# Values of two masked head groups in one 256-wide product, a new order of the filling work, and single weight buffers

## The chip, the cores and the metric

The kernel runs on one core of one Trainium2 chip. The metric is the device time of one execution in microseconds (us). Before the change it is 3708.43 us, the median of 3 runs (3707.75 to 3712.06). TensorE, VectorE, ScalarE and GpSimd are called PE, DVE, ACT and POOL, as in the profile; SP is the engine whose queue issues most loads.

## What is computed

Four attention layers act one after the other on `x` [4 batches, 512 queries, 256 channels]; each attends to the same context [4, 1024 keys, 512]. All of it is float32. Layers 0, 2 and 3 are "masked" layers of 16 heads of 64 channels:

```python
q, k, v = x @ Wq, ctx @ Wk, ctx @ Wv              # 1024 wide each, split into 16 heads of 64
logits = q . k * 64 ** -0.5 + col_bias            # the bias is nonzero at four token columns
x = softmax(logits) @ v (heads joined) @ Wo + bo + x
```

Layer 1 is "grouped": an RMS norm of x comes first, then 16 query heads of 16 channels share 4 key and value heads; its result is added to x as well. A batch needs its layers in order; different batches do not depend on each other.

## The kernel before, in words

**Groups and steps.** A masked layer of one batch is cut into 8 groups (`u` = 0..7) of two heads, 128 columns of Wq, Wk and Wv and 128 rows of Wo. Over 3 layers and 4 batches there are 96 masked groups, called `masked[0..95]`; `g.n` is a group's place in that list. The grouped layer of a batch is cut into 8 groups as well, 32 in all. Two strings written out by hand, `MASKED_TURNS` and `GROUPED_TURNS` (lines 56 to 63), say from which batch the next masked and the next grouped group come. Each character is one step, so step n always has masked group n, and 32 of the 96 steps have a grouped group too (12 to 19, 22 to 29, 32 to 39, 68 to 75).

**One step** (loop at line 960) writes out instructions in this order; every engine then works through its own in that order:

1. Loads for later steps go to SP's queue: `load_masked` (line 969) for groups n+3 (Wk), n+2 (Wq, Wv) and n-1 (Wo).
2. `scores(g)` (line 622): PE forms the logits of group n, eight blocks of 128 keys (lines 632, 638); ACT copies each block from PSUM to SBUF (line 642); DVE keeps a running maximum over the blocks (line 646).
3. `attend(g1)` (line 652, product in line 662) for the group before, whose exponentials are ready by now. In a step with a grouped group, its logits (line 611) lie between.
4. The softmax of group n on DVE, ACT and POOL runs beside all that follows: eight subtractions of the maximum (DVE, line 727), eight exponentials (ACT, line 733), seven running sums (POOL, line 772). They are listed as `events` with times and are written out between the pieces of the next item.
5. `fill` (lines 1108 to 1160) is a list of PE work for later steps: the output projections of earlier groups (line 831), queries (line 543), the keys of group n+2 (`k_part`, line 467: 16 matmul records of 512 columns), the grouped layer's own keys (line 485), the sum of squares of its norm (`rms_norm`, line 577, product in line 582), transposes of the next context (line 373), and, last, the values of group n+1 (`v_begin`, `v_end`, product in line 509: for each of 8 key blocks and 4 slices of the context, weights = a 128x128 piece of the context, moving = 128 columns of Wv; each float32 product shows as two records, so 64 records of 128 columns a group). Each item has a guessed duration; their sum `now` decides when events, and the `pairs` of maxima of the next grouped group (line 603), are put in between. `pair(0)` first writes out all events that are left.

In the step two ahead of a batch's grouped layer (steps 10, 20, 30 and 66) the fill also holds that layer's keys and norm. `rms_norm` needs squares from ACT (line 575), then PE sums them (line 582), ACT takes the root (line 586), and DVE turns it into a factor and multiplies (lines 565 to 567, 590). In the step after it the queries of the grouped layer use the result, and the four `pairs` begin.

**Buffers.** PSUM has 8 banks; `Place` (line 96) hands them out. The softmax holds two of them for the maxima (`mb_place`, given back after the eighth subtraction, line 729); a pair of grouped logits takes four. Wk and Wv have two buffers each of [128, 4, 128], keys and values two each.

**Start.** The first weights go out on SP's queue ahead of the masks: Wk of group 0, Wv of group 0, Wq of group 0, Wk of group 1. The context is gathered in four parts, transposed by PE and copied by ACT (line 379). The values of group 0 are made right after the scores of step 0 (line 1094).

Of the kernel before, what the change touches and what calls it, by code (L numbers as in the profile page):

```python
# [27 lines left out]
class Group:  # L28
# [7 lines left out]
    def __init__(self, **kw):  # L36
        self.__dict__.update(kw)
        self.masked = self.l != 1
        self.rows = [slice(64 * j, 64 * (j + 1)) for j in range(2)]
        self.name = f"{self.l}_{self.b}_{self.u}"  # L40


def units(b):
# [11 lines left out]

MASKED_TURNS = (
    "000000001111111122222222000000001111111100000000"
    "222222223333333311111111222223333333322233333333"
)
GROUPED_TURNS = (  # L60
    "............00000000..11111111..22222222........"
# [15 lines left out]
def kernel(ctx: ExitStack, tc: tile.TileContext, a: dict, out: bass.AP):  # L77
# [8 lines left out]
    def t_(shape, tag, name, bufs=1, dtype=FP):  # L86
        return sb.tile(shape, dtype, tag=tag, name=name, bufs=bufs)
# [305 lines left out]
    def w_tile(g, n, kk, bufs):  # L393
        return t_([P, kk, P], f"w{n}", f"w{n}_{g.name}", bufs=bufs)

    def load_k(g):
        if g.masked or g.first:
            g.wk = load_kv(g, "k")

    def load_kv(g, n):  # L400
        w = w_tile(g, n, KT, 2)
        if g.masked:
            nc.sync.dma_start(
                out=w,
                in_=a[f"L{g.l}_xattn_W{n}"][:, g.p * P : (g.p + 1) * P].rearrange("(k p) c -> p k c", p=P),
            )
        else:
            nc.gpsimd.memset(w, 0.0)
            for k in range(KT):
                nc.sync.dma_start(  # L410
                    out=w[:, k, :].rearrange("p (g d) -> p g d", d=32)[:, :, 0:16],
                    in_=a[f"L1_xattn_w{n}"][k * P : (k + 1) * P, :].rearrange("p (g d) -> p g d", d=16),
                )
        return w

    def load_v(g):
        if g.masked or g.first:
            g.wv = load_kv(g, "v")

    def load_q(g):  # L420
        if g.masked:
            g.wq = w_tile(g, "q", KC, 2)
            nc.sync.dma_start(
                out=g.wq,
                in_=a[f"L{g.l}_xattn_Wq"][:, g.p * P : (g.p + 1) * P].rearrange("(k p) c -> p k c", p=P),
            )
        elif g.h == 0:
            g.wq = w_tile(g, "q1", KC, 1)
            nc.gpsimd.memset(g.wq, 0.0)
            for k in range(KC):  # L430
                nc.sync.dma_start(
                    out=g.wq[:, k, :].rearrange("p (g d) -> p g d", d=32)[:, :, 0:16],
                    in_=a["L1_xattn_wq"][k * P : (k + 1) * P, :].rearrange(
                        "p (g r d) -> p g r d", r=4, d=16
                    )[:, :, g.r, :],
                )
# [15 lines left out]
    def k_half(g, n):  # L452
        k_part(g, n, 0)
        return k_part(g, n, 1)

    def k_part(g, n, part):

        if not g.masked:
            return k_grouped(g, n, part)
        if n == 0 and part == 0:  # L460
            g.kt = t_([P, T], "kt", f"kt_{g.name}", bufs=2)
        if part == 0:
            g.k_place = Place(1)
        w = g.k_place
        m = w.ap
        for k in (2 * part, 2 * part + 1):
            nc.tensor.matmul(  # L467
                m, lhsT=g.wk[:, k, :], rhs=ctx_t[g.b][:, k, n * 512 : (n + 1) * 512],
                start=(k == 0), stop=(k == KT - 1),
            )  # L470
        if part:
            return lambda: (nc.scalar.copy(g.kt[:, n * 512 : (n + 1) * 512], m), w.back())  # L472

    def k_grouped(g, h, part):

        if h == 0 and part == 0:
            g.kts = [t_([P, T // 2], f"kt1{i}", f"kt1{i}_{g.name}") for i in range(2)]
            g.kt = g.kts[0]
        if part == 0:
            g.k_place = Place(1)  # L480
        w = g.k_place
        m = w.ap
        for k in (2 * part, 2 * part + 1):
            for odd in range(2):
                nc.tensor.matmul(  # L485
                    m[64 * odd : 64 * (odd + 1), :], lhsT=g.wk[:, k, 64 * h : 64 * (h + 1)],
                    rhs=ctx_t[g.b][:, k, :].rearrange("p (i e q) -> p e i q", e=2, q=P)[:, odd],
                    start=(k == 0), stop=(k == KT - 1),
                )
        if part:  # L490
            return lambda: (
                nc.scalar.activation(g.kts[h], m, AF.Identity, bias=row16[:, 0:1]), w.back()
            )

    def v_half(g, n):
        v_begin(g, n)
        return v_end(g, n)

    def v_begin(g, n):
        if n == 0:  # L500
            g.v = t_([P, NT, P], "v" if g.masked else "v1", f"v_{g.name}", bufs=2 if g.masked else 1)
        g.v_place = Place(1)
        v_quarter(g, n, 0)

    def v_quarter(g, n, half):
        m = g.v_place.ap
        for t in range(2 * half, 2 * half + 2):
            for k in range(KT):
                nc.tensor.matmul(  # L509
                    m[:, t * P : (t + 1) * P],  # L510
                    lhsT=ctx_t[g.b][:, k, (4 * n + t) * P : (4 * n + t + 1) * P], rhs=g.wv[:, k, :],
                    start=(k == 0), stop=(k == KT - 1),
                )

    def v_end(g, n):
        v_quarter(g, n, 1)
        w = g.v_place
        m = w.ap

        def evacuate():  # L520
            nc.scalar.copy(g.v[:, 4 * n : 4 * n + 4, :], m.rearrange("p (t q) -> p t q", q=P))  # L521
            w.back()
            if not g.masked:

                v = g.v.rearrange("p t (g d) -> p t g d", d=32)
                nc.scalar.copy(
                    v[:, 4 * n : 4 * n + 4, :, 16:17],
                    ones[:, 0:16].rearrange("p (t g o) -> p t g o", t=4, o=1),
                )

        return evacuate

# [361 lines left out]
    def masked_at(n):  # L894
        return masked[n] if n < len(masked) else None
# [24 lines left out]
    def run(items):  # L920
        for _, w in items:
            done = w()
            if callable(done):
                done()
# [2 lines left out]
    order_keys()  # L927
    rests = [p() for p in parts[-1]]
    g0, g1 = masked[0:2]
    load_k(g0)  # L930
    load_v(g0)
    load_q(g0)
    load_k(g1)
    load_masks()
    make_keys()
    rests[1:1] = [lambda: project_q(g0)]
    rests[4:4] = [lambda: k_half(g0, 0)]
    for w in rests + [lambda: k_half(g0, 1)]:
        w()()
    load_k(masked[2])  # L940
    load_v(g1)
    load_q(g1)
    for l in (0, 2, 3):
        load_column(f"L{l}_xattn_bo")
# [2 lines left out]
    def keys(of):  # L947
        return [(1.7, lambda h=h, part=part: k_part(of, h, part)) for h in range(2) for part in range(2)]

    def values(of):  # L950
        return [(1.8, lambda h=h, part=part: part(of, h)) for h in range(2) for part in (v_begin, v_end)]

    attended = None
# [6 lines left out]
    for n in range(len(steps) + 2):  # L960
# [6 lines left out]
        rests = [p() for p in parts.get(n, ())] if n >= 0 else []  # L967

        def load_masked():
            if g and masked_at(g.n + 3):  # L970
                load_k(masked_at(g.n + 3))
            if g and masked_at(g.n + 2):
                load_q(masked_at(g.n + 2))
            if g1:
                load_o(g1)
            if g and masked_at(g.n + 2):
                load_v(masked_at(g.n + 2))

        def load_grouped():
            third = at(n + 3)[1]  # L980
            if third and third.first:
                load_k(third)
            if third and third.h == 0:
                load_q(third)
            if soon and soon.first:
                load_v(soon)
            if coming:
                load_o(coming)

# [96 lines left out]
        elif g1:  # L1086
# [4 lines left out]
            scale_out(g1)  # L1091
            for add in adds:
                add()
        if n == 0:
            run(values(g))
        if g:
            for t in range(NT):
                events.append((0.7 + 1.2 * t, lambda t=t: subtract(g, t)))
# [21 lines left out]
        if lam:  # L1120
# [6 lines left out]

            fill.append((3.6, attend_grouped))
            late.append(lambda: keep_odd(lam))
        kk = masked[1:3] if n == 0 else [masked_at(g.n + 2)] if g else []  # L1130
        for of in kk:
            fill += keys(of) if of else []
        if soon and soon.first:

            def square():
                behind_exponentials()
                norm_square(soon.b)

            of_keys = keys(soon)
            fill += of_keys[:3] + [(0.0, square)] + of_keys[3:]  # L1140
        fill += of_grouped
        if soon and soon.first:
            fill.append((1.7, lambda: rms_norm(soon.b, st_slot((NT + 1) * (count % 2) + NT))))
        fill += [(1.0, rest) for rest in rests]
        if coming and coming.first:
            fill += values(coming)
        if g and masked_at(g.n + 1):
            fill += values(masked[g.n + 1])
        if follows and follows.l and follows.u == 0:

            fill[-1:-1] = [(1.7, lambda: project_q(follows))]
# [27 lines left out]
            ready.append(g1)  # L1179
        if n == 0:  # L1180
            load_masked()
        load_grouped()
        for b in range(B):
            if left[b] == 0:
                left[b] = -1
# [24 lines left out]
```

## Time and profile before

| Quantity | us |
|---|---|
| median of 3 runs | 3708.43 |
| the profiled execution's own time | 3708.3 |
| its span | 3706.5 |
| PE busy (18606 matmul records) | 3675.1 |
| DVE busy | 2979.7 |
| ACT busy | 2109.5 |
| POOL busy | 1624.8 |
| PE in line 509, values (6400 records) | 753.9 |
| PE in line 467, masked keys (1536 records) | 686.7 |

The profile is of one execution. "Busy" of PE is a union of modelled matmul times: a matmul record lasts some 600 ns from its start to its end, while the next one starts earlier, so what a matmul costs is read from the distance between starts. PEld stands for the weight loads, which overlap with the matmuls. A row of the timeline merges neighbours of one kind: start, length from the first start to the last end, engine, line, tiles, shapes and the number of records; in brackets is the idle time ahead of it and what ended that.

### The profile page before, as it was taken

Reading aid. Unit: us, or ns where it says so; the run is one execution under the profiler, and the core shown is the slowest. Engines: PE = TensorE matmul, PEld = TensorE weight load, DVE = VectorE, ACT = ScalarE, POOL = GpSimd, SP = SyncE. Lnnn points to the kernel's source line nnn. Section 1 sums busy time; section 2 is a strip of 40 time slices with the busy share of each in tenths; the row PEclk is TensorE's granted clock in tenths of the full one; section 3 lists DMA queues with packets and bytes.
Section 4 is the critical chain, followed back from the end, with each engine's and each line's share of the span. In section 5 each row is a group of like instructions: output and inputs, shape, how many; then the busy total and the mean of one; then the engine's idle time right before and its main releaser. Section 6 shows DMA issues by size and latency. Waiting matters only on the chain.

```text
span 3706.5 us, 48343 instructions
## 1 busy us (share of the span) xinstructions
PE 3675.1 (99%) x18606; PEld 1835.8 (50%) x18606; DVE 2979.7 (80%) x3913; ACT 2109.5 (57%) x2433; POOL 1624.8 (44%) x749
## 2 busy tenths in 40 slices
PE   8999999999999999999999999999999999999998
PEld 4555544445444454444555555555544445555554
DVE  6777788878888788887887778788788878887887
ACT  4555565565555655556555555555555655555554
POOL 3555433333333333333454555555433334555554
PEclk9999999999999999999999999999999999999999
DMA  2111110001000010000000110000100010000100
GB/s 68 43 32 31 43 28 22 21 12 31 22 22 20 13 31 22 22 20 20 24 25 22 48 37 26 26 26 18 33 22 17 18 30 22 25 26 26 32 25 9
DMA packets 187868, 98.58 MB, mean 27 GB/s; under 512 B 43241, under 2 KB 183529, under 8 KB 187637
## 3 DMA queue, kind: packets, MB, share of 16 engines
q1 hardware_dynamic: 182510, 82.90, 8.2%
q0 software_dynamic: 2560, 8.39, 0.8%
q10 hardware_dynamic: 2566, 4.20, 0.5%
q8 instruction: 147, 2.41, 0.3%
q14 instruction: 85, 0.69, 0.1%
HBM read 89.16 MB, written 2.10 MB: 25 GB/s over the span
## 4 chain that ended last, share of the span: by engine, by line
PE 95%; DVE 3%; ACT 1%; issue 1%; DMA 0%; POOL 0%; ACTq 0%; DVEq 0%; POOLq 0%
PE ps L662 21%; PE ps L509 20%; PE ps L467 18%; PE ps L632 17%; PE ps L611 8%; PE ps L831 5%; PE ps L543 5%; DVE ps L646 1%; DVE st L727 1%; PE ps L485 1%; PE ps L638 1%; ACT st L642 0%; ACT st L619 0%; PE ps L373 0%; PE ps L582 0%
## 5 line engine op out<-in xcount | busy, mean ns | idle before, releaser
L772 POOL TENSOR_TENSOR st<-st 128x1024 f32<-128x1024 f32 x668 | 1580.3, 2366 | 2033.6 <-ACT st L733 1988.9
L646 DVE TENSOR_TENSOR ps<-ps,st 128x1024 f32<-128x1024 f32 x672 | 828.5, 1233 | 466.9 <-ACT st L642 404.4
L733 ACT ACTIVATE st<-st 128x1024 f32<-128x1024 f32 x768 | 785.2, 1054 | 432.1 <-DVE st L727 419.4
L727 DVE TENSOR_TENSOR st<-st,ps 128x1024 f32<-128x1024 f32 x768 | 882.3, 1215 | 3.2
L662 PE MATMUL ps<-st,v 128*64 128x512 f32 (+1 forms) x4064 | 810.9, 598 | 0.0
L509 PEld LDWEIGHTS ps<-wv,ctx 128*128 128x128 f32 x6400 | 732.8, 192 | 107.0 <-issue 76.9
L509 PE MATMUL ps<-wv,ctx 128*128 128x128 f32 x6400 | 753.9, 277 | 0.6 <-ACT st L642 0.6
L642 ACT COPY st<-ps 128x1024 f32<-128x1024 f32 x768 | 713.2, 1051 | 69.2 <-PE ps L638 68.4
L632 PE MATMUL ps<-qt,kt 64*128 64x512 f32 x3072 | 702.2, 596 | 1.3 <-ACT st L642 0.7
L467 PE MATMUL ps<-ctx,wk 128*128 128x512 f32 x1536 | 686.7, 597 | 2.2 <-ACT ctx L379 2.2
L662 PEld LDWEIGHTS ps<-st,v 128*64 128x64 f32 (+1 forms) x4064 | 231.2, 130 | 551.5 <-issue 468.1
L467 PEld LDWEIGHTS ps<-ctx,wk 128*128 128x128 f32 x1536 | 287.8, 190 | 388.9 <-issue 375.5
L632 PEld LDWEIGHTS ps<-qt,kt 64*128 64x128 f32 x3072 | 285.1, 186 | 324.5 <-ACT st L642 164.2
L521 ACT COPY v<-ps 128x512 f32<-128x512 f32 x200 | 117.0, 585 | 576.0 <-PE ps L509 575.8
L603 DVE TENSOR_TENSOR st<-st,ps 128x1024 f32<-128x1024 f32 x224 | 273.5, 1221 | 155.9 <-ACT st L601 90.2
L619 ACT ACTIVATE st<-ps 128x1024 f32<-128x1024 f32 x256 | 248.1, 1021 | 154.8 <-PE ps L611 127.0
L611 PE MATMUL ps<-qt,kt 32*128 32x512 f32 x2048 | 304.9, 639 | 2.5 <-DVE ot L813 1.2
L549 ACT ACTIVATE qt<-ps 128x512 f32<-128x512 f32 x96 | 56.9, 593 | 251.3 <-PE ps L543 251.3
L543 PE MATMUL ps<-x,wq 128*128 128x512 f32 x384 | 188.3, 613 | 1.1 <-ACT x L351 1.1
L831 PE MATMUL ps<-ot,wo 128*128 128x512 f32 x384 | 176.8, 602 | 4.3 <-ACT st L619 3.5
L611 PEld LDWEIGHTS ps<-qt,kt 32*128 32x128 f32 x2048 | 90.2, 182 | 159.8 <-ACT st L619 51.9
L472 ACT COPY kt<-ps 128x512 f32<-128x512 f32 x192 | 110.5, 575 | 49.2 <-PE ps L467 43.2
(144 smaller groups left out, 1575.7 us busy)
## 6 DMA issues: line engine op xcount, KB each, us to landing
wk<-in_L_xattn_Wk_dram SPq DMA_DIRECT2D x96, 256.0 KB, 3.0
wv<-in_L_xattn_Wv_dram SPq DMA_DIRECT2D x96, 256.0 KB, 2.8
wq<-in_L_xattn_Wq_dram SPq DMA_DIRECT2D x96, 128.0 KB, 2.9
wo<-in_L_xattn_Wo_dram SPq DMA_DIRECT2D x96, 128.0 KB, 2.9
qt<-qt ACTq DMA_DIRECT2D x32, 128.0 KB, 2.2
xraw<-in_x_dram SPq DMA_DIRECT2D x3, 512.0 KB
out_dram<-out SPq DMA_DIRECT2D x3, 512.0 KB, 3.3
wq<-in_L_xattn_wq_dram SPq DMA_DIRECT2D x32, 32.0 KB
```

The lines of the kernel that those rows point to most:

```text
L467: nc.tensor.matmul(m, lhsT=g.wk[:, k, :], rhs=ctx_t[g.b][:, k, n * 512 : (n + 1) * 512], start=(k == 0), stop=(k == KT - 1),)
L509: nc.tensor.matmul(m[:, t * P : (t + 1) * P], lhsT=ctx_t[g.b][:, k, (4 * n + t) * P : (4 * n + t + 1) * P], rhs=g.wv[:, k, :], start=(k == ...
L543: nc.tensor.matmul(m, lhsT=g.wq[:, k, :], rhs=x[:, k, :], start=(k == 0), stop=(k == KC - 1))
L611: nc.tensor.matmul(ws[odd].ap[:, j * S : (j + 1) * S], lhsT=g.kt[rows, i * P : (i + 1) * P], rhs=g.qt[rows, :], start=True, stop=True,)
L632: nc.tensor.matmul(m[:, j * S : (j + 1) * S], lhsT=g.kt[g.rows[j], keys], rhs=g.qt[g.rows[j], :], start=True, stop=t > 0,)
L642: nc.scalar.copy(g.st[t], m)
L646: nc.vector.tensor_tensor(top, top, g.st[t], ALU.max)
L662: nc.tensor.matmul(g.po[at, :], lhsT=g.v[:, t, rows], rhs=g.st[t][:, j * S : (j + 1) * S], start=(t == first), stop=(t == last),)
L727: nc.vector.tensor_tensor(g.st[t], g.st[t], g.mb, ALU.subtract)
L733: nc.scalar.activation(st, st, AF.Exp)
L772: nc.gpsimd.tensor_tensor(g.acc, g.st[0] if t == 1 else g.acc, g.st[t], ALU.add)
L831: nc.tensor.matmul(m[:, k * S : (k + 1) * S], lhsT=each.wo[:, k * P : (k + 1) * P], rhs=each.ot, start=each is g, stop=each is of[-1],)
```

## The change

- Two neighbouring masked groups (even n and n+1) must be of the same batch and layer; the second string of turns is reordered so that they always are (batch 2's last masked layer is split 6 and 2 instead of 5 and 3).
- Values: `v_pair` makes the values of both groups at once. The weights are the same 128x128 piece of the context, the moving side is 256 columns of Wv. A pair needs 64 records of 256 columns. This is done in the even step's fill, for the pair of which g itself is the first. Odd steps make no values; they make the keys of groups n+1 and n+2.
- In the fill the values now stand right behind the masked keys and ahead of the grouped layer's keys, square and norm, ahead of the transposes of the next context; output projections of grouped groups stand between the two halves of the values. The norm's sum and the context transposes are the last items of steps 10, 20, 30 and 66.
- Weights: Wk and Wv of a pair are one load of 512 KB into one buffer of [128, 4, 256] (one buffer, not two). Wk of the next pair is loaded at the head of an even step, Wv at the head of an odd one. The grouped layer's Wk and Wv use space that belongs to its values (`v1`) and its output (`o1`).
- Start: Wk is loaded in halves with Wq between, Wv of the first pair is issued on ACT's queue after two of four context parts and the first half of the keys; the values are no longer made ahead of the fill of step 0.

```diff
 MASKED_TURNS = (
     "000000001111111122222222000000001111111100000000"
-    "222222223333333311111111222223333333322233333333"
+    "222222223333333311111111222222333333332233333333"
 )
...
+    def load_pair(n, q, halves=(slice(0, 2),), queue=nc.sync):
+
+        g = masked[2 * q]
+        w = t_([P, KT, 2 * P], f"w{n}", f"w{n}_{g.name}")
+        for j, each in enumerate(masked[2 * q : 2 * q + 2]):
+            each.w[n] = w[:, :, j * P : (j + 1) * P]
+            each.w[n + "2"] = w
+
+        def part(of):
+            at = slice(of.start * P, of.stop * P)
+            queue.dma_start(
+                out=w[:, :, at],
+                in_=a[f"L{g.l}_xattn_W{n}"][:, (g.p + of.start) * P : (g.p + of.stop) * P].rearrange(
+                    "(k p) c -> p k c", p=P
+                ),
+            )
+
+        return [lambda of=of: part(of) for of in halves]
+
+    def load_grouped(g, n):
+
+
+        if n == "k":
+            w = t_([P, NT, P], "v1", f"wk_{g.name}")[:, 0:KT, :]
+        else:
+            w = t_([P, S], "o1", f"wv_{g.name}").rearrange("p (k c) -> p k c", c=P)
+        g.w[n] = w
+        nc.gpsimd.memset(w, 0.0)
...
+    def v_pair(g, n, half):
+
+        if n == 0 and half == 0:
+            pair_v = t_([P, NT, 2 * P], "v", f"v_{g.name}")
+            for j in range(2):
+                masked[g.n + j].v = pair_v[:, :, j * P : (j + 1) * P]
+            g.v2 = pair_v
+        if half == 0:
+            g.v_place = Place(1)
+        w = g.v_place
+        m = w.ap
+        t = 2 * n + half
+        for k in range(KT):
+            nc.tensor.matmul(
+                m[:, half * 2 * P : (half + 1) * 2 * P],
+                lhsT=ctx_t[g.b][:, k, t * P : (t + 1) * P], rhs=g.w["v2"][:, k, :],
+                start=(k == 0), stop=(k == KT - 1),
+            )
+        if half:
+            return lambda: (
+                nc.scalar.copy(
+                    g.v2[:, 2 * n : 2 * n + 2, :], m.rearrange("p (t q) -> p t q", q=2 * P)
+                ),
+                w.back(),
+            )
...
-    load_k(g0)
-    load_v(g0)
+    of_k = load_pair("k", 0, (slice(0, 1), slice(1, 2)))
+    of_k[0]()
     load_q(g0)
-    load_k(g1)
+    of_k[1]()
...
-    rests[4:4] = [lambda: k_half(g0, 0)]
+
+    rests[4:4] = [lambda: k_half(g0, 0), lambda: load_pair("v", 0, queue=nc.scalar)[0]]
     for w in rests + [lambda: k_half(g0, 1)]:
         w()()
-    load_k(masked[2])
-    load_v(g1)
     load_q(g1)
...
     def values(of):
+        if of.masked:
+            return [(1.8, lambda n=n, h=h: v_pair(of, n, h)) for n in range(NI) for h in range(2)]
...
         def load_masked():
-            if g and masked_at(g.n + 3):
-                load_k(masked_at(g.n + 3))
+
+
             if g and masked_at(g.n + 2):
+                if g.n % 2 == 0:
+                    load_pair("k", g.n // 2 + 1)[0]()
+                elif g.n > 0:
+                    load_pair("v", g.n // 2 + 1)[0]()
                 load_q(masked_at(g.n + 2))
             if g1:
                 load_o(g1)
-            if g and masked_at(g.n + 2):
-                load_v(masked_at(g.n + 2))
...
-        if n == 0:
-            run(values(g))
...
-        kk = masked[1:3] if n == 0 else [masked_at(g.n + 2)] if g else []
+        kk = masked[1:2] if n == 0 else masked[g.n + 1 : g.n + 3] if g and g.n % 2 else []
         for of in kk:
             fill += keys(of) if of else []
+
+        of_values = values(g) if g and g.n % 2 == 0 else []
+        fill += of_values[:4] + of_grouped + of_values[4:]
         if soon and soon.first:
...
             of_keys = keys(soon)
             fill += of_keys[:3] + [(0.0, square)] + of_keys[3:]
-        fill += of_grouped
-        if soon and soon.first:
             fill.append((1.7, lambda: rms_norm(soon.b, st_slot((NT + 1) * (count % 2) + NT))))
         fill += [(1.0, rest) for rest in rests]
         if coming and coming.first:
             fill += values(coming)
-        if g and masked_at(g.n + 1):
-            fill += values(masked[g.n + 1])
```

More of the change, by code (lines that the diff above doesn't have):

```diff
@@ L38, in __init__ @@
         self.masked = self.l != 1
+        self.w = {}
         self.rows = [slice(64 * j, 64 * (j + 1)) for j in range(2)]
@@ L394, in w_tile @@
         return t_([P, kk, P], f"w{n}", f"w{n}_{g.name}", bufs=bufs)
[L396 to L402, printed above, removed]
+    def load_pair(n, q, halves=(slice(0, 2),), queue=nc.sync):
[21 more added lines that the diff above has]
+        for k in range(KT):
             nc.sync.dma_start(
-                out=w,
-                in_=a[f"L{g.l}_xattn_W{n}"][:, g.p * P : (g.p + 1) * P].rearrange("(k p) c -> p k c", p=P),
-            )
[L407 to L418, printed above, removed]
+                out=w[:, k, :].rearrange("p (g d) -> p g d", d=32)[:, :, 0:16],
+                in_=a[f"L1_xattn_w{n}"][k * P : (k + 1) * P, :].rearrange("p (g d) -> p g d", d=16),
+            )
     def load_q(g):
@@ L467, in k_part @@
             nc.tensor.matmul(
-                m, lhsT=g.wk[:, k, :], rhs=ctx_t[g.b][:, k, n * 512 : (n + 1) * 512],
+                m, lhsT=g.w["k"][:, k, :], rhs=ctx_t[g.b][:, k, n * 512 : (n + 1) * 512],
                 start=(k == 0), stop=(k == KT - 1),
@@ L485, in k_grouped @@
                 nc.tensor.matmul(
-                    m[64 * odd : 64 * (odd + 1), :], lhsT=g.wk[:, k, 64 * h : 64 * (h + 1)],
+                    m[64 * odd : 64 * (odd + 1), :], lhsT=g.w["k"][:, k, 64 * h : 64 * (h + 1)],
                     rhs=ctx_t[g.b][:, k, :].rearrange("p (i e q) -> p e i q", e=2, q=P)[:, odd],
@@ L493, in k_grouped @@
             )
-    def v_half(g, n):
-        v_begin(g, n)
-        return v_end(g, n)
+    def v_pair(g, n, half):
[9 more added lines that the diff above has]
+        t = 2 * n + half
+        for k in range(KT):
+            nc.tensor.matmul(
[10 more added lines that the diff above has]
+            )
     def v_begin(g, n):
         if n == 0:
-            g.v = t_([P, NT, P], "v" if g.masked else "v1", f"v_{g.name}", bufs=2 if g.masked else 1)
+            g.v = t_([P, NT, P], "v1", f"v_{g.name}")
         g.v_place = Place(1)
@@ L510, in v_quarter @@
                     m[:, t * P : (t + 1) * P],
-                    lhsT=ctx_t[g.b][:, k, (4 * n + t) * P : (4 * n + t + 1) * P], rhs=g.wv[:, k, :],
+                    lhsT=ctx_t[g.b][:, k, (4 * n + t) * P : (4 * n + t + 1) * P], rhs=g.w["v"][:, k, :],
                     start=(k == 0), stop=(k == KT - 1),
@@ L522, in evacuate @@
             w.back()
[L523 to L529, printed above, removed]
+            v = g.v.rearrange("p t (g d) -> p t g d", d=32)
+            nc.scalar.copy(
+                v[:, 4 * n : 4 * n + 4, :, 16:17],
+                ones[:, 0:16].rearrange("p (t g o) -> p t g o", t=4, o=1),
+            )
         return evacuate
@@ L975, in load_masked, with load_others @@
                 load_o(g1)
-            if g and masked_at(g.n + 2):
-                load_v(masked_at(g.n + 2))
-        def load_grouped():
+        def load_others():
             third = at(n + 3)[1]
             if third and third.first:
-                load_k(third)
+                load_grouped(third, "k")
             if third and third.h == 0:
@@ L985, in load_grouped @@
             if soon and soon.first:
-                load_v(soon)
+                load_grouped(soon, "v")
             if coming:
@@ L1181 @@
             load_masked()
-        load_grouped()
+        load_others()
         for b in range(B):
```

## The prediction

> **What bounds the kernel now.** First the page: busy shares and the chain.
>
> ```profile
> PE 3675.1 (99%) x18606; PEld 1835.8 (50%) x18606; DVE 2979.7 (80%) x3913; ACT 2109.5 (57%) x2433; POOL 1624.8 (44%) x749
> PE 95%; DVE 3%; ACT 1%; issue 1%; DMA 0%; POOL 0%; ACTq 0%; DVEq 0%; POOLq 0%
> ```
>
> PE is 95% of the chain and hardly idle, so an edit counts if it changes what PE issues or makes PE wait. Next PE's timeline over one plain step, and the weight loads of its values:
>
> ```profile
> 250.13 7.03 PE L467 MATMUL ps<-ctx,wk 128*128 128x512 f32 x16
> 257.00 7.31 PE L509 MATMUL ps<-wv,ctx 128*128 128x128 f32 x64
> 264.23 1.13 PE L632 MATMUL ps<-qt,kt 64*128 64x512 f32 x4
> 297.89 1.13 PE L632 MATMUL ps<-qt,kt 64*128 64x512 f32 x4
> ```
>
> ```profile
> 257.00 7.11 PEld L509 LDWEIGHTS ps<-wv,ctx 128*128 128x128 f32 x63 [0.24 <-issue]
> ```
>
> From scores to scores the step lasts 33.66 us without an idle bracket. A key record (512 columns) costs (257.00 - 250.13)/16 = 429.4 ns. The 63 loads of the values start every (7.11 - 0.19)/62 = 111.6 ns, so a value record (128 columns) costs that; a group's values take 7.23 us, of which 0.09 is the switch to the scores. That switch stays, since keys before scores pay it too.
>
> Third, the groups by form, for the lengths of one record:
>
> ```profile
> L509 PE MATMUL ps<-wv,ctx 128*128 128x128 f32 x6400 | 753.9, 277 | 0.6 <-ACT st L642 0.6
> L467 PE MATMUL ps<-ctx,wk 128*128 128x512 f32 x1536 | 686.7, 597 | 2.2 <-ACT ctx L379 2.2
> L373 PE MATMUL ps<-ident,craw 128*128 128x128 f32 x96 | 12.5, 274 | 0.0
> ```
>
> The value group waits 0.6 us in all: nothing is to be won but its pitch.
>
> **The change part by part.**
>
> *Wider values.* Per pair 128 records of 128 columns (14.28 us) become 64 of 256. No row has 256 columns, so I bracket. Upper end: no gain per column, 2 x 111.6 = 223.2 ns. Lower end: the transposes (L373) also move 128 columns, and eight take 1.04 us from first start to last end, hence (1.04 - 0.27)/7 = 110 ns, 109.4 unrounded; a line through that and the keys' 429.4 gives 216.1 at 256. A line through values and keys gives 111.6 + 128 x 0.8276 = 217.5. I take 216.1: the values' extra 2 ns over a transpose look like their slower weight load (192 against 141 ns), and the keys' equally slow load (190) is covered by 512 columns. So 64 x 216.1 = 13.83 us, 0.455 less per pair, 48 pairs: -21.8 us (217.5: -17.5; 223.2: 0).
>
> The Trainium skill speaks for much more ("TensorE: Matmul & The Clock Gate", Back-to-back issue gap): with weights loaded for every matmul, 128 columns take about 81 ns instead of 56, so 25 ns for the load. With 3072 loads gone that would be an estimated 77 us. The trace denies it: the whole excess over a transpose is about 2 ns. I use the row.
>
> *Order of keys and values.* An even step has 13.8 us of values, an odd one 2 x 6.87 us of keys, instead of 6.87 + 7.14 in each: the steps stay level. ACT evacuates four banks of 512 columns in either case. Priced at 0. A layer's first query now stands ahead of the last four key records (1.72 us) instead of half a group of values (3.6). ACT needs 0.59 for it and its exponentials end some 27 us into a step, so 0 too; without that cover at most 1 us in each of 8 steps.
>
> *Single buffers.* The skill ("Trainium Kernel Development and Optimization", Best Practices) says to double-buffer so that loads lie beside work, which speaks against the change. By the rows it costs nothing: a 256 KB load lands in 3.0 us (4.4 at worst), so I allow 9 for 512 KB; Wk's last reader is in one odd step, its next reader in the next, with a whole even step (30.2 us at least), scores and attention (14.3) between, 44 us. What could eat this is SP's queue: its longest wait is for POOL's clearing of a grouped Wo, and Wk stands right behind it:
>
> ```profile
> SPq L447 <- POOL wo L444: 712.6, 16, 45.5
> ```
>
> ```profile
> 593.78 1.72 SPq L447 DMA_DIRECT2D wo<-in_L_xattn_wo_dram x4
> 595.60 0.39 SPq L403 DMA_DIRECT2D wk<-in_L_xattn_Wk_dram x1
> ```
>
> But the wait began early; it ends at 593.8, and the step it loads for begins with scores at 595.8. Over 30 us of slack remain, for Wv likewise: 0. The grouped weights' clearing (POOL, 0.52 us) moves to space whose readers are done before it or, for `o1`, in the same step; POOL's next sums come only 17 us into the step: 0.
>
> *The norm is moved to the end.* This is the part that costs. Before, a group's values (7.2 us) follow the norm's product; afterwards the next scores do (in step 10 with 0.88 us of transposes between). PE and DVE around step 21's start:
>
> ```profile
> 859.35 1.88 PE L582 MATMUL ps<-xn,ones 128*128 128x512 f32 x4
> 861.07 7.31 PE L509 MATMUL ps<-wv,ctx 128*128 128x128 f32 x64
> 868.30 1.13 PE L632 MATMUL ps<-qt,kt 64*128 64x512 f32 x4
> 895.14 2.37 PE L611 MATMUL ps<-qt,kt 32*128 32x512 f32 x8 [0.25 <-DVE st L727]
> ```
>
> ```profile
> 863.84 3.70 DVE L590 SCALAR_TENSOR_TENSOR xn<-x,colL_xattn_norm_w,inv 128x512 f32<-128x512 f32 x2
> 871.69 9.26 DVE L646 TENSOR_TENSOR ps<-ps,st 128x1024 f32<-128x1024 f32 x7 [4.15 <-ACT st L642]
> 889.25 5.74 DVE L727 TENSOR_TENSOR st<-st,ps 128x1024 f32<-128x1024 f32 x5
> ```
>
> DVE ends the norm at 867.54, 8.19 us after L582 starts (ACT's root in between), and is then free until the maxima at 871.69, 3.39 after the scores. Afterwards L582 starts 1.72 before the scores, so the norm ends 8.19 - 1.72 = 6.47 behind them, and the maxima, which are queued behind it, start 3.08 late. From there to the last subtraction (894.99) DVE has no gap, and the first grouped logits on PE already wait for that subtraction, which frees the two banks. So PE loses 3.08. The same rows for steps 30 and 66 give 8.18 - 1.71 - 3.39 = 3.08 and 8.11 - 1.82 - 3.40 = 2.89; for step 10, 8.08 - 1.82 - 0.88 - 3.38 = 2.00. Sum +11.0 us (0 if the lag is caught up before the logits). Square, keys and root themselves keep their length, and the square comes some 7 us later behind the exponentials, so nothing waits for it.
>
> *End and start.* ACT at the end:
>
> ```profile
> 3659.86 2.95 ACT L733 ACTIVATE st<-st 128x1024 f32<-128x1024 f32 x3
> 3662.72 7.40 ACT L642 COPY st<-ps 128x1024 f32<-128x1024 f32 x8
> ```
>
> The last scores start at 3660.29; copies elsewhere follow 1.43 later (868.30, 869.73), here 2.43, because step 94 is only 24.4 us long and the exponentials are behind. Afterwards step 94 holds the whole pair's values, step 0 correspondingly less, so the lag goes: -1.0 (0 to -1.8, PE's waits there). At the start Wv's issue on ACT (some 0.5 us) stands between the key copy (to 27.86) and the context copy (28.14): +0.2 (0 to 0.5); it lands near 32, the values come near 50.
>
> Sum: -21.8 + 11.0 - 1.0 + 0.2 = -11.6. The profiled execution took 3708.3 (span 3706.5 and 1.8 around it), so 3696.7; on the median of 3708.4, 3696.8: 3697 us.
>
> **The rivals.**
>
> 1. *The norm stays hidden.* DVE or PE catches up before the grouped logits: the sum is -22.6, 3686 us. For it: DVE is idle 20% overall. Against: no gap in that stretch, and PE already waits there.
> 2. *The records hardly get cheaper.* At 217.5 ns the sum is -7.3 (3701), at 223.2 +10.2 (3719); break-even is near 219.7. The edit then does not do what it says, and the norm's cost is left. Against it: keys at 0.839 ns a column, values at 0.872.
> 3. *Weights come late*, slower than before. With one buffer, PE stands in the key or value item until the load has landed. There are 94 reloads, so each us past the slack costs 94 us: 0.12 us on average eats the gain, 0.4 us gives 3735. For it: SP waits up to 45.5 us for POOL. Against: those waits end at the step's boundary, 30 us ahead of the use.
>
> **How the numbers follow.** My sum 0.50; rival 1 0.20; rival 2 0.20; rival 3 0.10. About 0.2% (7.4 us) is what a measurement can tell from no change, so 3701.0 and 3715.8 are the borders. Nearly all of the first two is faster, 0.69; of rival 2 most lies between, with a bit of my sum 0.18; rival 3 and the worst of rival 2 slower, 0.13. The range 3683 to 3707 takes in rival 1 and most of rival 2; the sum alone spans 3692 to 3702.
>
> **What would show it.** Value records of 256 columns 216 ns apart (217.5 or more: rival 2); plain odd steps near 33.4 and even ones near 30.0 us; in steps 11, 21, 31 and 67 the maxima starting some 6.5 us behind the scores and PE waiting 2 to 3 us longer at the first L611 (no longer: rival 1); no PE wait on a load of Wk or Wv (else rival 3); the last score copies 1.4 us behind their scores. A stall spread over the 32 grouped steps, 0.4 us each, would undo the sum.

## The result and the profile after

The changed kernel takes 3693.0 us (median of 6 runs, 3691.07 to 3694.2); the kernel before, run beside it, 3709.24 (3707.75 to 3712.36, 6 runs). The ratio is 0.9954, 95% interval 0.9941 to 0.9967: faster by 16 us, where 11.6 were forecast. The profiled execution took 3692.11 us, its span is 3690.3 instead of 3706.5.

The page of the changed kernel, busy shares and chain (PE still carries it, with 3072 records less):

```profile
PE 3656.6 (99%) x15534; PEld 1709.0 (46%) x15534; DVE 2970.3 (80%) x3912; ACT 2112.2 (57%) x2433; POOL 1622.7 (44%) x749
PE 94%; DVE 3%; ACT 1%; issue 1%; DMA 0%; POOL 0%; ACTq 0%; DVEq 0%; POOLq 0%
```

PE's timeline over two plain steps (line 519 makes the values of a pair, 478 the keys, 664 the scores), and the weight loads of those values:

```profile
243.28 13.98 PE L519 MATMUL ps<-wv,ctx 128*128 128x256 f32 x64
257.19 1.13 PE L664 MATMUL ps<-qt,kt 64*128 64x512 f32 x4
276.74 13.90 PE L478 MATMUL ps<-ctx,wk 128*128 128x512 f32 x32
290.57 1.13 PE L664 MATMUL ps<-qt,kt 64*128 64x512 f32 x4
```

```profile
243.28 13.57 PEld L519 LDWEIGHTS ps<-wv,ctx 128*128 128x128 f32 x63 [0.24 <-issue]
```

A 256-column record costs (13.57 - 0.19)/62 = 215.8 ns from start to start. The odd step lasts 290.57 - 257.19 = 33.38 us, without a wait, where the same kind of step lasted 33.66.

The groups by form: the values wait for nothing, and the 256-column record is 382 ns long from start to end. (Lengths are not one figure: 277 ns at 128 columns and 597 at 512 in the kernel before.)

```profile
L519 PE MATMUL ps<-wv,ctx 128*128 128x256 f32 x3072 | 690.3, 382 | 0.0
```

The loads, 512 KB each on SP's queue (last number: us from issue to landing). They are issued at the head of a step and used a step later:

```profile
wk<-in_L_xattn_Wk_dram SPq DMA_DIRECT2D x47, 512.0 KB, 3.5
wv<-in_L_xattn_Wv_dram SPq DMA_DIRECT2D x47, 512.0 KB, 3.6
```

PE and DVE around the start of step 21, where the norm's product (line 614) now stands right ahead of the scores (lines 622 the norm's multiply, 678 the maxima, 759 the subtractions, 643 the grouped logits):

```profile
857.13 1.98 PE L614 MATMUL ps<-xn,ones 128*128 128x512 f32 x4
859.04 1.13 PE L664 MATMUL ps<-qt,kt 64*128 64x512 f32 x4
886.58 2.37 PE L643 MATMUL ps<-qt,kt 32*128 32x512 f32 x8 [0.95 <-DVE st L759]
```

```profile
861.82 1.42 DVE L622 SCALAR_TENSOR_TENSOR xn<-x,colL_xattn_norm_w,inv 128x512 f32<-128x512 f32 x2
863.15 9.25 DVE L678 TENSOR_TENSOR ps<-ps,st 128x1024 f32<-128x1024 f32 x7
880.70 5.73 DVE L759 TENSOR_TENSOR st<-st,ps 128x1024 f32<-128x1024 f32 x5
```

The maxima start 4.11 us behind the scores, not 3.39 as before and not 6.47 as forecast: DVE's norm is over at 863.24. The bracket at the grouped logits grew from 0.25 to 0.95 us, by as much as the maxima are late.

Last, ACT's copies of the last scores, which start at 3645.14:

```profile
3646.58 7.43 ACT L674 COPY st<-ps 128x1024 f32<-128x1024 f32 x8 [1.76 <-PE ps L670]
```

They follow 1.44 us behind (2.43 before).

**Where the 16.2 us of span came from.** From the first scores of step 0 to those of step 95, the 95 steps are 16.39 us shorter. Of that, 48 pairs win some 0.475 each: -22.8. The four steps behind a norm (11, 21, 31, 67) and step 10 are longer by 4.7 than the pairs' gain would make them: 0.77, 0.71, 0.43, 2.56 and 0.22. Some 1.7 is spread over other steps, 0.1 each in some of those that transpose a context and in some just behind them, 0.3 in step 49; it was not traced. From the last scores to the end: 46.2 us before, 45.2 after, -1.05. The first scores start at 34.99 instead of 33.75, +1.24.

### The profile page after: what moved, and what is told of

Its sections match the earlier page's. It is cut to its first block, busy times and chain, and to the rows that moved or that the text cites. A ratio compares the mean times of both kernels' runs of the same rounds, so it can differ in the third digit from the quotient of the medians.

```text
span 3690.3 us, 42021 instructions
## 1 busy us (share of the span) xinstructions
PE 3656.6 (99%) x15534; PEld 1709.0 (46%) x15534; DVE 2970.3 (80%) x3912; ACT 2112.2 (57%) x2433; POOL 1622.7 (44%) x749
## 4 chain that ended last, share of the span: by engine, by line
PE 94%; DVE 3%; ACT 1%; issue 1%; DMA 0%; POOL 0%; ACTq 0%; DVEq 0%; POOLq 0%
PE ps L694 21%; PE ps L519 18%; PE ps L478 18%; PE ps L664 17%; PE ps L643 8%; PE ps L863 5%; PE ps L575 5%; DVE ps L678 1%; DVE st L759 1%; PE ps L542 1%; PE ps L496 1%; PE ps L670 1%; ACT st L651 0%; PE ps L374 0%; ACT st L674 0%
## 5 line engine op out<-in xcount | busy, mean ns | idle before, releaser
L519 PE MATMUL ps<-wv,ctx 128*128 128x256 f32 x3072 | 690.3, 382 | 0.0
L519 PEld LDWEIGHTS ps<-wv,ctx 128*128 128x128 f32 x3072 | 577.1, 190 | 152.5 <-issue 57.3
L526 ACT COPY v<-ps 128x512 f32<-128x512 f32 x192 | 111.6, 583 | 248.2 <-PE ps L519 247.5
```

The source lines that it names most:

```text
L519: nc.tensor.matmul(m[:, half * 2 * P : (half + 1) * 2 * P], lhsT=ctx_t[g.b][:, k, t * P : (t + 1) * P], rhs=g.w["v2"][:, k, :], start=(k = ...
```

## The experiments

Six timed variants were run beside the kernel before, and one was executed once. Theory A: the gain is the price of the value records; the norm at the end costs only what its short chain shows. The rivals were that the new order brings the gain (B), and that the norm costs the 11 us of the prediction (C).

**Two narrow products.** Everything stays in its new place, but each product is split:

```diff
-        for k in range(KT):
-            nc.tensor.matmul(
-                m[:, half * 2 * P : (half + 1) * 2 * P],
-                lhsT=ctx_t[g.b][:, k, t * P : (t + 1) * P], rhs=g.w["v2"][:, k, :],
+        for j in range(2):
+            for k in range(KT):
+                nc.tensor.matmul(
+                    m[:, (2 * half + j) * P : (2 * half + j + 1) * P],
+                    lhsT=ctx_t[g.b][:, k, t * P : (t + 1) * P],
+                    rhs=g.w["v2"][:, k, j * P : (j + 1) * P],
...
```

> The changed kernel with everything in its new place, but each 256-wide value product made as two 128-wide ones (128 value records a pair instead of 64). Theory A (the gain is the price of the value records): records 111.6 ns apart, 48 x (128 x 111.6 - 64 x 215.8) = +23 us over the changed kernel, so about 3716 us, 6 to 7 us slower than before. Rival B (the new order of keys and values, not the width, brings the gain): stays near 3693.

Measured: 3714.34 us (3713.3 to 3718.51, 11 runs), ratio to before 1.0016 (1.0007 to 1.0025). The values of one pair as weight loads:

```profile
245.15 14.26 PEld L520 LDWEIGHTS ps<-wv,ctx 128*128 128x128 f32 x127 [0.24 <-issue]
```

They start (14.26 - 0.19)/126 = 111.7 ns apart again. The whole gain is gone, and the new order (with the norm at its end) is by itself slower than the old. Step by step against the changed kernel, every even step is 0.46 to 0.48 us longer and no plain odd one is; steps 21 and 67 lose 1.65 more, by a halved clock (below). B falls.

**The norm between the halves of the values.**

```diff
-        fill += of_values[:4] + of_grouped + of_values[4:]
+        fill += of_values[:4] + of_grouped
...
             fill.append((1.7, lambda: rms_norm(soon.b, st_slot((NT + 1) * (count % 2) + NT))))
+        fill += of_values[4:]
```

> The changed kernel with the grouped keys, the square and the norm of steps 10, 20, 30 and 66 put between the two halves of the values, so that 6.9 us of values follow the norm's product. Theory A (the norm at the end costs only its visible stalls, some 3 us, plus 1.7 us of halved clock in step 67): 3688 to 3690 us, the maxima of steps 11, 21, 31, 67 start 3.4 us behind the scores again, the multiply of the norm takes 1.7 us again instead of 0.75. Rival C (the norm at the end costs the 11 us of my prediction and the values win more than their records show): about 3682 us.

Measured: 3689.66 us (3688.96 to 3689.99, 5 runs), ratio to before 0.9948 (0.9935 to 0.9962), so 3.3 us under the changed kernel's median. The two were not run side by side and the intervals of their ratios overlap; the steps carry the reading. Steps 21 and 31 are shorter by 0.70 and 0.69, step 67 by 2.56; step 11 is longer by 2.04, of which 1.65 is a halved clock. The maxima of steps 21, 31 and 67 start 3.4 us behind the scores again, as A expected; those of step 11 do not, they start 4.53 behind. The multiply is slow again (mean of one, ahead of it the busy sum):

```profile
L622 DVE SCALAR_TENSOR_TENSOR xn<-x,colL_xattn_norm_w,inv 128x512 f32<-128x512 f32 x8 | 11.7, 1506 | 0.4
```

So the norm's place costs about 3 us, not 11.

**The kernel before with the norm last.** The reverse: the block that appends `rms_norm` stands behind `fill += values(masked[g.n + 1])`, nothing else is changed.

> The kernel before with one edit: the norm's product and its multiply moved behind the values, to the very end of the fill of steps 10, 20, 30 and 66. Theory A: the chain behind the product is 6.1 us long, not 8.2, so the maxima start 0.7 us late; +3 us (2 to 5, the more if a clock window is lost): about 3712 us. Rival C: +11 us: 3720.

Measured: 3716.63 us (3714.25 to 3717.9, 11 runs), ratio 1.0018 (1.0009 to 1.0027): 7.8 us slower, more than A expected and less than C. The chain behind the product, in step 20:

```profile
867.63 1.88 PE L582 MATMUL ps<-xn,ones 128*128 128x512 f32 x4
872.30 1.42 DVE L590 SCALAR_TENSOR_TENSOR xn<-x,colL_xattn_norm_w,inv 128x512 f32<-128x512 f32 x2
873.63 9.25 DVE L646 TENSOR_TENSOR ps<-ps,st 128x1024 f32<-128x1024 f32 x7
```

It is 872.30 + 1.42 - 867.63 = 6.09 us long, as A said. In the profile steps 11, 21, 31 and 67 are longer by 0.99, 2.45, 0.79 and 1.00; 1.65 of step 21's 2.45 is a halved clock. So 3.6 us are waits and 1.65 clock. Another 1.0 lies in steps 24, 41, 62 and 77 and 0.2 at the start, untraced; the further 1.3 by which the median exceeds the 6.5 us between the two profiled spans stay open.

**Fewer running sums.** In the kernel before, POOL's sums are cut to the first of seven in the four steps with a norm (the softmax sums of those four groups are incomplete):

```diff
-        if t < g.now:
+        if t < g.now and (t == 1 or g.n not in (10, 20, 30, 66)):
             running_sum(g, t)
```

> The kernel before with six of seven running sums on POOL left out in steps 10, 20, 30 and 66, so the softmax sums of those four groups are incomplete. Theory D (the norm's multiply, which reads two operands from SBUF, is slow in the kernel before because POOL's running sums read SBUF at the same time): it falls from 1.67 to 0.75 us each, in its old place. Rival E (it is slow because of what PE and ACT do in that place): stays at 1.67. The total stays within 2 us of before in either case, since values hide it.

One execution: 3712.18 us (span 3710.4, 3.9 us over the span before, so not within the 2 us expected; two halved clock windows, in steps 11 and 67, account for 3.25 of it). The norm's multiply, in its old place, first in the kernel before and then here:

```profile
L590 DVE SCALAR_TENSOR_TENSOR xn<-x,colL_xattn_norm_w,inv 128x512 f32<-128x512 f32 x8 | 13.1, 1674 | 0.3
```

```profile
L590 DVE SCALAR_TENSOR_TENSOR xn<-x,colL_xattn_norm_w,inv 128x512 f32<-128x512 f32 x8 | 5.7, 749 | 0.4
```

D holds, E falls: the multiply takes longer when POOL's sums run beside it. In step 20 of the kernel before they last until 866.99 and cover all but the end of the two multiplies (863.84 to 867.54). In the changed kernel they are over at 857.58, before the multiplies start at 861.82 (first the kernel before, then the changed one):

```profile
854.55 12.44 POOL L772 TENSOR_TENSOR st<-st 128x1024 f32<-128x1024 f32 x5
```

```profile
852.78 4.80 POOL L804 TENSOR_TENSOR st<-st 128x1024 f32<-128x1024 f32 x2
```

This is what the Trainium skill states in "SBUF — State Buffer" (Who interferes with whom): a DVE instruction with two SBUF inputs contends with a GpSimd instruction that reads SBUF. The trace agrees: the multiply reads x and inv from SBUF, POOL's sums read st, and the price here is 1674 against 749 ns, both the mean of eight.

**The first pair of maxima later.** PE's wait at the first pair of grouped logits was there before the change too (brackets of 0.25 to 0.45 us in steps 11, 21 and 67, and more within the pair: 2.37 us for what takes 1.14 without a wait), and the norm only lengthens it. So the pair was moved by 3.4 us of keys or values, in three kernels: with the norm between, in the changed kernel as it is, and in the kernel before.

```diff
-            pairs += [((12.0 if lam else 11.0 if g else 0.0) + 2.5 * i, i) for i in range(NT // 2)]
+            pairs += [((12.0 if lam else 14.0 if g else 0.0) + 2.5 * i, i) for i in range(NT // 2)]
```

> The changed kernel with the norm between the halves of the values and, besides, the first pair of grouped maxima in steps 11, 21, 31 and 67 listed at 14.0 instead of 11.0, so that PE does some 3.4 us of keys before it needs the banks of the softmax's maxima. Theory A: the wait at the first pair (about 1.5 us in each of four steps: 0.3 ahead of it and 1.2 within it) is gone and with it the windows of halved clock that only these steps show (about one an execution, 1.65 us): 3682 to 3684 us, no half-clock window in the records between start and end. Rival F (the wait only moves to a later pair, or to the grouped logits of the next step): stays at 3688 to 3690.

Measured: 3682.36 us (3681.84 to 3683.29, 5 runs), ratio 0.9927 (0.9913 to 0.994). As A expected; no halved clock between start and end; F falls.

> The changed kernel as it is (the norm last), with the first pair at 14.0. Theory A: the norm's lag of 0.7 us disappears in the same 3.4 us, so the place of the norm costs nothing: as fast as the version with the norm between the values, 3682 to 3684. Rival C (a lag of some 3 us in each of the four steps that also shows elsewhere): 3 us or more slower than that version.

Measured: 3680.5 us (3678.01 to 3681.17, 5 runs), ratio 0.9921 (0.9907 to 0.9934), the fastest version: 12.5 us under the changed kernel's median with one number edited. The norm stands last here, and it costs nothing that shows: the time is even 1.9 us under the version with the norm between, below the expected 3682 to 3684. (Step 11 is 0.98 us shorter than in that version, steps 41 and 77 by 0.52 each; not traced.) Step 21 of this kernel:

```profile
854.24 1.98 PE L614 MATMUL ps<-xn,ones 128*128 128x512 f32 x4
877.43 8.75 PE L478 MATMUL ps<-ctx,wk 128*128 128x512 f32 x20
886.11 1.14 PE L643 MATMUL ps<-qt,kt 32*128 32x512 f32 x8
```

Twenty key records instead of twelve stand ahead of the first pair, the pair waits for nothing and takes 1.14 us instead of 2.37. Steps 11, 21 and 31 are 2.2 to 2.5 us shorter than in the changed kernel, step 67 is 4.3.

> The kernel before with the first pair at 14.0 and nothing else. Theory A: it wins the same waits and windows, some 6 us: about 3702. Against the changed kernel with the same edit this leaves the wider values, the level steps and the end of the kernel: 48 x 0.47 + 1.0 = 23.5 us less some 1 us. Rival B (order, not width): the difference is that of before and after, 16.

Measured: 3706.83 us (3704.24 to 3707.94, 11 runs), ratio 0.9991 (0.9982 to 1.0): 2.4 us instead of some 6, and hardly clear of no change. Steps 21, 31 and 67 are shorter by 1.55, 1.86 and 1.75, but in step 11 the later pair falls behind the transposes of a context and waits for ACT's copy of them, and the clock is halved behind that (+2.31). Step 41 is longer by 0.82 as well, not traced. The second half of the pair in step 11:

```profile
436.01 1.13 PE L611 MATMUL ps<-qt,kt 32*128 32x512 f32 x4 [1.36 <-ACT ctx L379]
```

Against this kernel the changed one with the same edit is 26.3 us faster: 22.8 from the records, 1.0 from the end, 4.0 from step 11 (48.25 us against 52.54, less a plain odd step's gain), where the longer run of keys keeps the pair ahead of the transposes, and 0.8 from step 41, less some 1.9 spread over other steps and not traced. That is 26.7; rival B's 16 is out.

## Why the prediction was right, and where a step was off

- **Wider values** (-21.8, mechanism right, size right): the line from transposes to keys gave 216.1 ns; measured 215.8, so -22.8 us with 0.475 a pair. Splitting the product takes 0.46 to 0.48 us a pair back. Rival 2 is out. Each of the 3072 records that went saved 2 x 111.6 - 215.8 = 7.4 ns, not the estimated 25 ns for its weight load that the prediction worked out from the Trainium skill ("TensorE: Matmul & The Clock Gate", Back-to-back issue gap), which would have made 77 us. The prediction was right to go by the rows, but one of its reasons was weak: the transposes load weights for every record too (96 loads for 96 records), so the 2 ns by which values exceed them are not the price of a load. Whether the 7.4 ns belong to the load or to the record is not separated here.
- **Order of keys and values** (0): plain odd steps 33.38 and even ones 30.03 us against forecasts of 33.4 and 30.0. Of the eight steps that make a layer's first query, seven are at most 0.14 us longer than the pairs' gain makes them; the eighth, step 31, carries the norm's wait.
- **Single buffers** (0): right; PE waits for no load of Wk or Wv after the start. Rival 3 is out.
- **The norm at the end** (+11.0): the place and the chain were right, DVE late, PE waiting at the first grouped logits, but the size was off. The mis-sized term is the 8.19 us from the norm's product to the end of DVE's multiply. It was taken over from the old place, where the two multiplies took 3.70 us because POOL's sums read SBUF at the same time; in the new place the sums are done and the two take 1.42, so the chain is 6.11 us. The product also starts 1.91 ahead of the scores, not 1.72. Then the norm ends 6.11 - 1.91 = 4.20 behind the scores, the maxima at 4.11, 0.72 late instead of 3.08; step 21 is 0.71 longer than the pairs' gain makes it. All four steps: 2.8 us of waits, instead of 11.0. The price of a delay was right: maxima 0.72 late, PE 0.71 longer. A sign was in the profile: the multiply has the shape of the query correction in line 709 (752 ns) and took 1674.
- **What was not in the sum**: behind PE's wait in step 67 its clock was halved for 3.41 us, some 1.65 us lost. With this and 0.2 in step 10 the norm's cost in the profiled execution is 4.7, 6.3 less than forecast. The span's sum (-16.2 against -11.6) then closes: -6.3 for the norm, -1.0 for the values, +1.0 for the start, +1.7 not traced. That the sum missed by no more than 4.6 is in part luck: the norm's waits were priced 8.2 us too high and the values' gain 1.0 too low, and the clock window, step 10, the start and the untraced 1.7, none of them in the sum at that size, gave back 4.6 of these 9.2.
- **End** (-1.0): measured -1.05, and the copies start 1.44 behind the last scores. **Start** (+0.2): measured +1.24, which need not come from the change: first scores start anywhere from 33.7 to 35.5 us in the profiled executions of kernels with the old start and from 34.1 to 35.7 with the new one.
- **The range** took in rival 1, at 3686, and the result lies between the sum and that: the norm is neither hidden nor as late as forecast. With its wait hidden by later pairs the time even is 3680.5, since the old wait goes too.
- **Two slips of arithmetic** change nothing: rival 2 breaks even at 219.9 ns, not 219.7, and rival 3's 0.4 us give 3734, not 3735.

## What to carry to other kernels

On a kernel whose chain is nearly all PE, price a wider moving side from start-to-start distances of records in the trace, at two widths; a record's length is no measure of that (382 ns long here, 215.8 apart). A duration is only as good as its surroundings: before moving an instruction, ask what ran beside it, and compare it with another of its shape. When a change lengthens an existing wait, look at the wait itself: letting PE do a few more records before it needs the banks was worth 12.5 us in the changed kernel, three quarters of what the large change had brought, but only 2.4 in the kernel before, where the later pair ran into another wait.

## What the runs showed of the hardware that was not expected

PE's granted clock fell to half for a window of 3.41 us (in one case two on end) behind a short wait. In the changed kernel's step 67 PE waits 1.35 us for a bank:

```profile
2643.31 2.49 PE L643 MATMUL ps<-qt,kt 32*128 32x512 f32 x8 [1.35 <-DVE st L759]
2645.73 3.51 PE L478 MATMUL ps<-ctx,wk 128*128 128x512 f32 x4
2649.17 1.14 PE L643 MATMUL ps<-qt,kt 32*128 32x512 f32 x8
```

and in the view by stretches (after the busy times of PE, PEld, DVE, ACT and POOL comes PE's clock) the four key records behind it, 3.51 us instead of 1.98, lie in the slow one:

```profile
2645.40:2648.80 3.40, 3.40 (x5) 1.17 (x4) 3.10 (x6) 1.91 (x3) 3.24 (x3) 0.50 0.00 0
2648.80:2652.00 3.20, 3.20 (x13) 0.99 (x12) 1.55 (x2) 0.58 (x1) 3.12 (x2) 0.99 0.00 0
```

Apart from each execution's start and end, the nine profiled executions show such windows only in steps 11, 21 and 67, each within 3 us behind a wait at the first pair. The two versions without the wait in those steps show none. But longer waits pass without a window and shorter ones do not. Step 67 of the kernel before with the norm last (wait 1.45 us, key records at their usual length), then with few sums (0.44 us, key records slow):

```profile
2666.35 2.37 PE L611 MATMUL ps<-qt,kt 32*128 32x512 f32 x8 [1.45 <-DVE st L727]
2668.66 1.99 PE L467 MATMUL ps<-ctx,wk 128*128 128x512 f32 x4
```

```profile
2662.60 2.37 PE L611 MATMUL ps<-qt,kt 32*128 32x512 f32 x8 [0.44 <-DVE st L727]
2664.90 3.35 PE L467 MATMUL ps<-ctx,wk 128*128 128x512 f32 x4
```

In the profiled execution of the kernel before, waits of 0.25 to 0.45 us passed without one. That the wait takes part in the cause fits all nine executions, but it is not shown, and what decides between one wait and the next was not tried.
